# Graph-attention kernel: centring the linear weights 14 slots later in the last superblock of pass one, and spreading their sums from slot 42 to slot 66

## The chip, the cores and the metric

The kernel runs on one core of one Trainium2 chip. The metric is the time of one execution on the device, in microseconds (us). Before the change three runs gave 2664.1, 2664.25 and 2662.74 us, with a median of 2664.1 us.

## The reference

The input is x, 128 x 64 x 768, seen as 8192 tokens in 128 graphs of 64, and a 0/1 adjacency per graph. After a layer norm and a relu, two graph-attention layers follow. Everything is float32.

```python
for l in range(L):                                   # L = 2, H = 768
    m_left  = einsum('bsh,oh->bso', h, W_left[l])
    m_right = einsum('bsh,oh->bso', h, W_right[l])
    u_left  = einsum('bih,bjh->bij', h, m_left)  / sqrt(H)
    u_right = einsum('bih,bjh->bij', h, m_right) / sqrt(H)
    u = u_left * adj_tri + u_left * diag_mask + u_right * adj_tri.T
    e = exp(u) * adj
    attention = e / (e.sum(axis=2, keepdims=True) + 1e-10)
    h_lin = einsum('bsh,oh->bso', h, W_lin[l]) + b_lin[l]
    h = relu(layer_norm(matmul(attention, h_lin), ln_a[l], ln_b[l]))
return x + h
```

## The kernel before, in words

Each layer has two passes. **Pass one** multiplies the tokens by W_left and W_right, forms the scores and the softmax, and stores the attention. **Pass two** multiplies the tokens by W_lin, then by the attention, and normalizes. Both passes replace block products by a bilinear scheme with fewer products: sums of weight blocks times sums of token blocks, each product then added with signs into several outputs.

Pass one works through 32 parts of 256 tokens in 11 superblocks: the first of two parts, ten of three. One superblock after the first is 40 products (`PRODUCTS`), each of four matmuls at L658 into one of four PSUM banks in turn (names X, Y, Z, V or C, D, X, Y), so product i can start only when the reads of product i - 4 are done. The reads add each bank into the tiles m0, m1 and m2 (`READS`): the first write of a piece is a ScalarE activation (ACT) at L859, every later one a VectorE (DVE) operation at L245 or L863. After product 3 stand the score matmuls (L680) of the superblock before. The token sums that the products need (`T_OPS`, 38 of them, t9 to t46) are made one by one on GpSimd (POOL), at most 11 ahead of their use. L245 is the line of the helper `added`, so it stands for every addition on DVE and POOL; POOL and DVE additions on tiles g are sums of weights or tokens in SBUF, DVE additions on tiles m are reads of a bank.

The side work is put into a plan by slot: two slots per product, slot 2i while product i is issued and slot 2i + 1 behind its reads. `put(slot, f)` says at which slot f is written into the program; the engines then execute in their own order, each strictly in the order written. A slot is about 0.86 us when nothing waits.

In the **last superblock** of pass one (once in each layer), `final_of` adds the preparation of pass two to the plan:

- the nine blocks of W_lin are loaded (`load_n`, L214, slots 6 to 22), the first two token parts of pass two are loaded at slot 12, and the bias in three pieces (L901, slots 29 to 31);
- `centre` takes each row's mean out of W_lin, so that the layer norm of pass two needs no mean. The blocks go in three groups of three (j = 1, 0, 2), seven steps a group: for each block ACT copies the two halves onto themselves and accumulates their row sums (L233), DVE reduces the six sums and scales them (L228, L229), and ACT subtracts the mean from each block's halves (L237);
- `sums_n` makes the 17 weight sums of `W_SUMS` (n = 0 to 16), the even n on POOL, the odd n on DVE. Many work in place and so wait for each other across the two engines: n = 2 on POOL overwrites block 8, which n = 1 on DVE reads; n = 8 on POOL overwrites the block that n = 7 on DVE reads; n = 9 on DVE overwrites what n = 8 on POOL reads;
- the bias is summed, centred and combined at slots 40 to 60 (ACT L916, DVE L919 and L920, ACT L924, DVE L927 and L928, ACT L931);
- in the second layer ACT also applies scale, bias and relu to the first token parts (L379, 12 activations, slots 24 to 34);
- from slot 56 on POOL makes the 11 token sums of pass two (`put_sums_t`).

Around it stand the eight softmax steps of the superblock before at slots 10 to 31 (DVE L702 to L720, ACT L708), the last of which issues eight stores of the attention on the SP queue (L725), and the load of the next adjacency at slot 48, four DMA issues on ACT's own queue (L645).

Of the kernel before, what the change touches and what calls it, by code (L numbers as in the profile page):

```python
# [17 lines left out]
def kernel(  # L18
# [48 lines left out]
    def put(slot, *fs):  # L67
        plan.setdefault(slot, []).extend(fs)

    def put_all(slot, fs, step=1):  # L70
        for f in fs:
            if f is not None:
                put(slot, f)
            slot += step
        return slot
# [133 lines left out]
    def load_n(l):  # L209
        t = W[l, "n"] = {}  # L210

        def load(s, i, j):
            t[s] = free.popleft()
            nc.sync.dma_start(t[s], block_of("n", l, i, j))  # L214

        return [lambda s=s, ij=ij: load(s, *ij) for s, ij in RAW.items()]

    def centre(l):

        t = W[l, "n"]  # L220
        steps = []
        for j in (1, 0, 2):
            blocks = [s for s, (_, jj) in RAW.items() if jj == j]
            m = stat.tile([P, 3, K2], F32, name="wm", bufs=3)
            mean = stat.tile([P, K2], F32, name="wmm", bufs=3)

            def mean_of(m=m, mean=mean):
                nc.vector.reduce_sum(mean, m.rearrange("p n c -> p c n"), axis=mybir.AxisListType.X)  # L228
                nc.vector.tensor_scalar_mul(mean, mean, -1.0 / H)  # L229

            def sums(s, n, m=m):
                for c in range(K2):
                    nc.scalar.activation(t[s][:, c, :], t[s][:, c, :], AF.Copy, accum_out=m[:, n, c:c + 1])  # L233

            def less(s, mean=mean):
                for c in range(K2):
                    nc.scalar.activation(t[s][:, c, :], t[s][:, c, :], AF.Identity, bias=mean[:, c:c + 1])  # L237

            steps.extend([lambda n=n, s=s, sums=sums: sums(s, n) for n, s in enumerate(blocks)])
            steps.append(mean_of)  # L240
            steps.extend([lambda s=s, less=less: less(s) for s in blocks])
        return steps

    def added(eng, o, sign, a, b):
        (eng.tensor_add if sign == "+" else eng.tensor_sub)(o, a, b)  # L245

    def sums_n(l):
        t = W[l, "n"]

        def one(n, o, s, a, b):  # L250
            if o not in t:
                t[o] = free.popleft()
            added((nc.gpsimd, nc.vector)[n % 2], t[o], s, t[a], t[b])

        return [lambda n=n, x=x: one(n, *x) for n, x in enumerate(W_SUMS)]
# [27 lines left out]
    def put_sums_t(key, first, step, base):  # L283

        fs = sums_t(key)
        put_all(first, fs[:5], step)
        for f, s in zip(fs[5:], (21, 22, 23, 24, 25, 27)):
            put(max(base + s, first + 5 * step), f)
# [81 lines left out]
    def load_h(which, l, u, hold=False):  # L370
        for t in range(2):
            load_part(which, l, 2 * u + t, hold)
# [10 lines left out]
    def affine(which, l, u, step=1):  # L383
        return [lambda a=a, b=b: (a(), b()) for a, b in zip(*(affine_part(which, l, 2 * u + t, step) for t in range(2)))]
# [518 lines left out]
    def bias(l):  # L903


        ab = [free.popleft() for _ in range(2)]
        W[l, "bias"] = ab
        t = rows["bias", l] = [ab[n // 2][:, n % 2, :] for n in range(4)]
        todo = [lambda i=i, to=to: row(f"b{i}", b_lin[l], i * D, (i + 1) * D, t[to]) for i, to in enumerate((1, 2, 0))]
        bm = stat.tile([P, 3], F32, name="bm", bufs=1)  # L910

        bs = stat.tile([P, 1], F32, name="bs", bufs=1)

        def sums():
            for n in range(3):
                nc.scalar.activation(t[n], t[n], AF.Copy, accum_out=bm[:, n:n + 1])  # L916

        def mean():
            nc.vector.reduce_sum(bs, bm, axis=mybir.AxisListType.X)  # L919
            nc.vector.tensor_scalar_mul(bs, bs, -1.0 / H)  # L920

        def centred():
            for n in range(3):
                nc.scalar.activation(t[n], t[n], AF.Identity, bias=bs)  # L924

        def combined():
            nc.vector.tensor_add(t[1], t[1], t[0])  # L927
            nc.vector.tensor_add(t[3], t[1], t[2])  # L928

        def negated(n):  # L930
            nc.scalar.activation(t[n], t[n], AF.Copy, scale=-1.0)  # L931

        return todo, [sums, mean, centred, combined, lambda: negated(0), lambda: negated(2)]
# [322 lines left out]
    def final_of(l):  # L1256
        def final(slot, tokens):
            put_all(slot + 6, load_n(l), 2)
            put(slot + 12, lambda: load_h(2, l, 0))

            def rest():
                loads, work = bias(l)
                put_all(slot + 29, loads, 1)
                put_all(slot + 40, work, 4)

            put(slot + 28, rest)
            put_all(slot + 24, affine(2, l, 0), 2)
            put_all(slot + 14, centre(l), 1)
            put_all(slot + 30, sums_n(l), 2)
            put_sums_t((2, l, 0), slot + 56, 2, slot + 50)  # L1270
        return final

# [33 lines left out]
```

## Time and profile before

| | |
|---|---|
| median of 3 runs | 2664.1 us |
| profiled execution, its own time | 2660.78 us |
| span in the profile, first to last instruction | 2659.0 us |
| granted TensorE clock, mean | 0.996 |
| PE busy / DVE busy / POOL busy / ACT busy | 98% / 66% / 65% / 35% |
| last superblock, first layer | about 778 to 862 us |
| last superblock, second layer | about 2086 to 2169 us |

Views by time print one row per run of like instructions: start in us, duration in us, engine, line, operation, output <- input, count, and in square brackets how long the engine sat idle before it and which instruction released it. PE is the matrix engine. A product of four float32 matmuls stands there as eight records of 128x256. Views by group print busy time and mean ns of one, then the idle time before them. "issue" as a releaser means that no wait in the profile explains the idle time.

### The profile page before, as it was taken

To read this page: it belongs to the slowest core of one execution; us is meant where nothing else is said; L and a number is where in the kernel's file an instruction comes from. 1 tells how busy PE (TensorE), PEld (TensorE's weight loads), DVE (VectorE), ACT (ScalarE), POOL (GpSimd) and SP (SyncE) were. 2 spreads that over 40 slices of the span, in tenths; PEclk is the share of its full clock that TensorE was granted. 3 is DMA by queue.
4 is the path that set the end of the run, shared out by engine and by line. 5 is a ranking of instruction groups with operands and counts; after the bars stand their busy time and mean duration, and the time that the engine had idled before them with its cause. 6 is when DMAs were issued, how large, how long until landed. Compare 5 with 4: busy or idle time off the path is not lost. (4 is left out here: it accounts for less than half of the span.)

```text
span 2659.0 us, 46920 instructions
## 1 busy us (share of the span) xinstructions
PE 2602.9 (98%) x18042; PEld 2219.6 (83%) x18042; DVE 1753.8 (66%) x2840; ACT 934.3 (35%) x1963; POOL 1726.7 (65%) x1328
## 2 busy tenths in 40 slices
PE   9899999999999999999999999999999989999998
PEld 8788888888887788888788888888888878888886
DVE  7877787777768445554415676677666675666667
ACT  5522223223213254454542222222222425455453
POOL 4766676666668557776225666667666567878786
PEclk9999999999999999999999999999999999999999
DMA  7443534343421344446795524353542215565655
GB/s 219 111 112 87 123 92 113 92 116 78 100 62 52 123 148 151 163 136 215 203 287 137 130 60 111 77 128 93 133 100 69 66 49 150 160 172 159 182 159 146
DMA packets 263358, 336.52 MB, mean 127 GB/s; under 512 B 56290, under 2 KB 195298, under 8 KB 263138
## 3 DMA queue, kind: packets, MB, share of 16 engines
q1 hardware_dynamic: 246338, 325.28, 44.5%
q10 hardware_dynamic: 16800, 8.26, 1.2%
q8 instruction: 144, 2.36, 0.4%
q14 instruction: 76, 0.62, 0.1%
HBM read 218.11 MB, written 115.34 MB: 125 GB/s over the span
## 5 line engine op out<-in xcount | busy, mean ns | idle before, releaser
L245 POOL TENSOR_TENSOR g<-ht 128x512 f32<-128x512 f32 x584 | 769.1, 1327 | 474.4 <-ACT ht L379 117.6
L245 POOL TENSOR_TENSOR g<-g,g 128x512 f32<-128x512 f32 x295 | 381.9, 1303 | 140.1 <-DVE g L245 39.3
L245 POOL TENSOR_TENSOR g<-ht,g 128x512 f32<-128x512 f32 x256 | 338.1, 1328 | 156.3 <-PE X L658 40.0
L658 PE MATMUL C<-g,g 128*128 128x256 f32 x1008 | 241.1, 382 | 10.0 <-POOL g L245 8.0
L954 PE MATMUL Z<-g,g 128*128 128x256 f32 x1024 | 244.1, 380 | 2.8 <-ACT hl L300 2.7
L658 PE MATMUL X<-g,g 128*128 128x256 f32 x1008 | 241.3, 383 | 4.9 <-DVE m L863 4.8
L658 PEld LDWEIGHTS C<-g,g 128*128 128x128 f32 x1008 | 191.1, 191 | 39.3 <-POOL g L245 11.1
L658 PE MATMUL Y<-g,g 128*128 128x256 f32 x912 | 217.3, 381 | 3.8 <-POOL g L245 3.8
L954 PEld LDWEIGHTS Z<-g,g 128*128 128x128 f32 x1024 | 191.6, 190 | 35.1 <-issue 4.1
L379 ACT ACTIVATE ht<-ht,b_col,a_col 128x256 f32<-128x256 f32 x384 | 196.5, 592 | 67.5 <-DMA ht<-h 59.5
L658 PEld LDWEIGHTS X<-g,g 128*128 128x128 f32 x1008 | 192.0, 191 | 33.5 <-DVE m L863 5.6
L658 PE MATMUL D<-g,g 128*128 128x256 f32 x880 | 209.2, 381 | 3.2 <-POOL g L245 3.2
L658 PE MATMUL Z<-g,g 128*128 128x256 f32 x864 | 204.7, 380 | 0.0
L658 PEld LDWEIGHTS Y<-g,g 128*128 128x128 f32 x912 | 174.3, 191 | 28.1 <-POOL g L245 4.2
L245 DVE TENSOR_TENSOR m<-m,D 128x512 f32<-128x512 f32 x180 | 118.2, 677 | 117.6 <-ACT m L859 99.2
L658 PEld LDWEIGHTS D<-g,g 128*128 128x128 f32 x880 | 167.6, 191 | 27.0 <-POOL g L245 4.0
L658 PEld LDWEIGHTS Z<-g,g 128*128 128x128 f32 x864 | 163.5, 190 | 23.1
L954 PE MATMUL X<-g,g 128*128 128x256 f32 x768 | 182.7, 379 | 0.0
L658 PE MATMUL V<-g,g 128*128 128x256 f32 x768 | 181.4, 379 | 0.0
L1154 POOL TENSOR_TENSOR z<-z,b 128x768 f32<-128x768 f32 x62 | 112.7, 1829 | 81.7 <-DVE z L1151 77.2
L954 PEld LDWEIGHTS X<-g,g 128*128 128x128 f32 x768 | 145.7, 190 | 20.6 <-issue 0.6
L658 PEld LDWEIGHTS V<-g,g 128*128 128x128 f32 x768 | 145.9, 190 | 19.8
(224 smaller groups left out, 4661.9 us busy)
## 6 DMA issues: line engine op xcount, KB each, us to landing
ht<-h SPq DMA_DIRECT2D x126, 768.0 KB, 6.2
h<-xb SPq DMA_DIRECT2D x124, 384.0 KB, 6.5
z<-z SPq DMA_DIRECT2D x128, 192.0 KB, 3.1
x<-z SPq DMA_DIRECT2D x128, 192.0 KB, 5.4
xr<-in_x_dram SPq DMA_DIRECT2D x120, 192.0 KB, 3.8
out_dram<-xr SPq DMA_DIRECT2D x120, 192.0 KB, 2.7
x<-in_x_dram SPq DMA_DIRECT2D x112, 192.0 KB, 5.5
g<-form SPq DMA_DIRECT2D x40, 256.0 KB, 5.1
```

The source lines that it names most:

```text
L245: (eng.tensor_add if sign == "+" else eng.tensor_sub)(o, a, b)
L379: nc.scalar.activation(ht, ht, AF.Relu, bias=cols[1][:, c:c + 1], scale=cols[0][:, c:c + 1])
L658: nc.tensor.matmul(p[:, g], w[:, c, g * P:(g + 1) * P], t[:, c, :], start=(new and g == c == 0), stop=(c == K2 - 1), skip_group_check=True)
L954: nc.tensor.matmul(p[:, n], b[t][:, c, r * P:(r + 1) * P], w[s][:, c, :], start=(i in FIRST and i not in PRELOAD and n == c == 0), stop=(c ...
L1154: nc.gpsimd.tensor_add(zs[k], zs[k], rows["b"])
```

## The change

In both layers the 21 steps of `centre` move from slots 14 to 34 to slots 28 to 48. The 17 sums, before at every second slot from 30 to 62, now stand at slots 42, 43, 45, 46, 48, 49 and so on to 66.

```diff
             put(slot + 28, rest)
             put_all(slot + 24, affine(2, l, 0), 2)
-            put_all(slot + 14, centre(l), 1)
-            put_all(slot + 30, sums_n(l), 2)
+            put_all(slot + 28, centre(l), 1)
+            for n, f in enumerate(sums_n(l)):
+                put(slot + 42 + 3 * n // 2, f)
             put_sums_t((2, l, 0), slot + 56, 2, slot + 50)
```

No instruction is added or removed apart from regrouping; the 51 weight and token tiles g are handed out from a queue, so their numbers change from here on.

On POOL in the first layer's last superblock, these were the rows from the sum n = 0 (`g_119` is block 8, `g_153` block 12, `g_150` block 13) on; rows with ht are token sums or sums of token sums:

```order
L245 TENSOR_TENSOR g_163<-g_119,g_153 128x512
L245 TENSOR_TENSOR g_123<-ht,g_146 128x512
L245 TENSOR_TENSOR g_119<-g_119,g_150 128x512
L245 TENSOR_TENSOR g_143<-ht,g_129 128x512
L245 TENSOR_TENSOR g_157<-g_133,g_162 128x512
L245 TENSOR_TENSOR g_144<-ht 128x512
L245 TENSOR_TENSOR g_160<-g_152,g_121 128x512
```

With the change the same place on POOL reads:

```order
L245 TENSOR_TENSOR g_163<-ht,g_146 128x512
L245 TENSOR_TENSOR g_123<-ht,g_129 128x512
L245 TENSOR_TENSOR g_127<-ht 128x512
L245 TENSOR_TENSOR g_143<-g_152,g_121 128x512
L245 TENSOR_TENSOR g_157<-g_155,g_121 128x512
L245 TENSOR_TENSOR g_144<-g_119,g_153 128x512
L245 TENSOR_TENSOR g_160<-ht 128x512
L245 TENSOR_TENSOR g_151<-ht,g_130 128x512
L245 TENSOR_TENSOR g_119<-g_119,g_150 128x512
L245 TENSOR_TENSOR g_154<-ht,g_121 128x512
```

Before, the sum n = 2 (`g_119<-g_119,g_150`) stood behind token sum t35 and ahead of t36; now it stands behind t41, that is behind six more token sums, and n = 0 stands behind t39.

On DVE at the same time, in the difference (minus before, plus now), `g_142<-g_142,g_119` is the sum n = 1, `g_127<-g_163,g_150` and `g_135<-g_144,g_150` are n = 3 under its old and its new tile, `g_129<-g_147,g_162` is n = 7, and m rows are reads of banks:

```order
 L228 TENSOR_REDUCE wmm<-wm 128x2
 L229 TENSOR_SCALAR wmm<-wmm 128x2
-L245 TENSOR_TENSOR g_142<-g_142,g_119 128x512
 L863 TENSOR_SCALAR m_290<-C,m_290 128x8x64 x2
 L245 TENSOR_TENSOR m_290<-m_290,C 128x8x64
 L245 TENSOR_TENSOR m_288<-m_288,D 128x8x64
 L245 TENSOR_TENSOR m_290<-m_290,D 128x8x64
-L245 TENSOR_TENSOR g_127<-g_163,g_150 128x512
 L863 TENSOR_SCALAR m_290<-X,m_290 128x8x64
 L245 TENSOR_TENSOR m_290<-m_290,X 128x8x64
+L228 TENSOR_REDUCE wmm<-wm 128x2
+L229 TENSOR_SCALAR wmm<-wmm 128x2
```

The first pair L228, L229 is the mean of group j = 2 before and that of j = 1 now; n = 1 goes behind the reads of products 16 to 21, n = 3 behind those of product 22, and the means of j = 0 and j = 2 now stand between reads of products 18 and 23.

On ACT, these rows now stand between the centring of group j = 0 (`g_150`, `g_164`, `g_147`) and the read of product 25 (`m_289<-D`), the next bank read that ACT does:

```order
L916 ACTIVATE g_161,bm<-g_161 128x256 x2
L916 ACTIVATE g_122,bm<-g_122 128x256
L237 ACTIVATE g_147<-g_147,wmm 128x256 x2
L233 ACTIVATE g_133,wm<-g_133 128x256 x2
L233 ACTIVATE g_162,wm<-g_162 128x256 x2
L233 ACTIVATE g_128,wm<-g_128 128x256 x2
L237 ACTIVATE g_133<-g_133,wmm 128x256 x2
L237 ACTIVATE g_162<-g_162,wmm 128x256 x2
L645 DMA adj<-in_adj_dram 64x2x128 x2
L645 DMA adj<-in_adj_dram 64x4x128 x2
L237 ACTIVATE g_128<-g_128,wmm 128x256 x2
L924 ACTIVATE g_161<-g_161,bs 128x256 x2
```

Before, all of the centring stood ahead of the bias sums (L916) and of the four adjacency issues (L645); now the bias sums stand ahead of group j = 2, and the adjacency issues ahead of its last block.

## The prediction

> **What bounds the kernel now.** I read the page first: PE is busy 98% of the span, so only PE's waits can be won. Next came the timeline of PE. A superblock that nothing disturbs is the one ahead of the last in the first layer; these are its products 4 and 39.
>
> ```profile
> PE 2602.9 (98%) x18042; PEld 2219.6 (83%) x18042; DVE 1753.8 (66%) x2840; ACT 934.3 (35%) x1963; POOL 1726.7 (65%) x1328
> 716.23 1.99 PE L658 MATMUL X<-g,g 128*128 128x256 f32 x8
> 776.77 1.89 PE L658 MATMUL V<-g,g 128*128 128x256 f32 x8
> ```
>
> 35 products take 60.54 us, 1.73 each. In the last superblock the same products (first layer: 4, 20, 30, 39; second layer: 5, 20, 30, 39) stand so:
>
> ```profile
> 792.34 1.99 PE L658 MATMUL C<-g,g 128*128 128x256 f32 x8
> 821.70 1.99 PE L658 MATMUL C<-g,g 128*128 128x256 f32 x8 [1.47 <-POOL g L245]
> 843.44 3.65 PE L658 MATMUL X<-g,g 128*128 128x256 f32 x8 [2.38 <-DVE m L863]
> 860.77 1.89 PE L658 MATMUL Y<-g,g 128*128 128x256 f32 x8
> 2099.88 1.89 PE L658 MATMUL D<-g,g 128*128 128x256 f32 x8
> 2130.24 3.62 PE L658 MATMUL C<-g,g 128*128 128x256 f32 x8 [3.45 <-POOL g L245]
> 2151.97 1.99 PE L658 MATMUL X<-g,g 128*128 128x256 f32 x8 [2.37 <-DVE m L863]
> 2167.81 1.89 PE L658 MATMUL Y<-g,g 128*128 128x256 f32 x8
> ```
>
> First layer: 68.4 us for 35 products, 7.9 lost. Second: 67.9 for 34 where 58.8 would do, 9.1 lost. So **17.0 us** is all that this change can win. It is lost in two places: at product 20 for POOL, and at product 30, where bank X is still unread by DVE. After a wait PE sometimes runs one product at half speed (3.65 and 3.62 instead of 1.9), but not always (1.99).
>
> Why POOL is late is seen on POOL, DVE and ACT (POOL first layer, then second; then DVE):
>
> ```profile
> 819.15 1.27 POOL L245 TENSOR_TENSOR g<-g,g 128x512 f32<-128x512 f32 x1 [7.85 <-DVE g L245]
> 820.39 1.26 POOL L245 TENSOR_TENSOR g<-ht,g 128x512 f32<-128x512 f32 x1
> 2127.67 1.27 POOL L245 TENSOR_TENSOR g<-g,g 128x512 f32<-128x512 f32 x1 [10.67 <-DVE g L245]
> 817.99 0.12 DVE L228 TENSOR_REDUCE wmm<-wm 128x2 f32<-128x6 f32 x1
> 818.22 0.69 DVE L245 TENSOR_TENSOR g<-g,g 128x512 f32<-128x512 f32 x1
> ```
>
> By the order of rows, 819.15 is sum n = 2, 818.22 is n = 1, which it waits for, and n = 1 stands behind the mean of group j = 2 (817.99). Behind n = 2 is token sum t36 (820.39 to 821.65), and product 20 starts at 821.70. POOL idles 7.85 and 10.67 us, then runs without a gap, late.
>
> **The change part by part.** It adds no work. It moves 36 copies and subtractions on ACT, three means on DVE, nine sums on POOL and eight on DVE; it issues no DMA itself, and SP's queue keeps its order. The prices:
>
> ```profile
> L233 ACT ACTIVATE g<-g 128x256 f32<-128x256 f32 x18 | 7.2, 408 | 0.0
> 818.41 2.50 ACT L237 ACTIVATE g<-g,wmm 128x256 f32<-128x256 f32 x6 [0.65 <-DVE wmm L229]
> L379 ACT ACTIVATE ht<-ht,b_col,a_col 128x256 f32<-128x256 f32 x24 | 12.6, 598 | 0.0
> L229 DVE TENSOR_SCALAR wmm<-wmm 128x2 f32<-128x2 f32 x3 | 1.6, 549 | 0.1
> L245 DVE TENSOR_TENSOR g<-g,g 128x512 f32<-128x512 f32 x8 | 10.8, 1348 | 2.8 <-POOL g L245 2.8
> 864.13 2.47 DVE L245 TENSOR_TENSOR m<-m,X 128x512 f32<-128x512 f32 x4
> 866.52 2.47 DVE L245 TENSOR_TENSOR m<-m,Y 128x512 f32<-128x512 f32 x4
> ```
>
> A group's six copies take 2.4 us, its six subtractions 2.5, one L379 0.5 start to start, a read of a bank 0.60 (four in 2.39). A mean and its way back to ACT cost about 0.5 us, or 1.2 where L229 is slow. A DVE sum takes 0.69 us with POOL idle (818.22), 1.35 on average. A bank can be read 1.95 us after its product's start.
>
> *POOL.* Undisturbed, product i starts at 792.4 + 1.73 (i - 4). With the change t35 to t39 come ahead of every sum, then n = 0 once block 12 is centred, t40, t41, then n = 2, which still waits for n = 1. From this walk: ACT reads product 13, which starts at 808.0, three times by 811.4 and copies j = 1 by 813.8; DVE reaches the mean after the transposition at 815.7; ACT subtracts from 816.2 to 818.6 and copies j = 0 by 821.0. DVE waits for that from 820.2, reads products 19 to 21 by 824.4, and does n = 1 by 825.0. POOL then does n = 2 and t42 by 827.7, t43 by 829.0; products 26 and 27 want them at 830.4 and 832.2. **The wait at product 20 goes in both layers** (second layer: t42 at 2134.1 for 2136.2), with about 2 us to spare; if that cover is gone, product 26 waits for the excess.
>
> *DVE and ACT, the new path.* What is late next is bank X at product 30. Rows for it (ACT, ACT's DMA queue, then SP, then DVE):
>
> ```profile
> 826.61 0.42 ACT L916 ACTIVATE g<-g 128x256 f32<-128x256 f32 x1 [5.70 <-DMA g<-in_b_lin_dram]
> 828.08 1.28 ACTq L645 DMA_DIRECT2D adj<-in_adj_dram  x2
> 2052.22 1.58 ACT L379 ACTIVATE ht<-ht,b_col,a_col 128x256 f32<-128x256 f32 x3 [1.50 <-issue]
> 837.07 0.60 ACT L859 ACTIVATE m<-D 128x512 f32<-128x512 f32 x1 [6.17 <-DVE m L863]
> 818.10 5.09 SPq L725 DMA_DIRECT2D att<-wm  x8
> 823.23 0.59 SPq L901 DMA_DIRECT2D g<-in_b_lin_dram  x1
> 838.30 1.67 DVE L245 TENSOR_TENSOR g<-g,g 128x512 f32<-128x512 f32 x1
> 839.90 1.48 DVE L927 TENSOR_TENSOR g<-g 128x256 f32<-128x256 f32 x1
> 841.42 1.37 DVE L928 TENSOR_TENSOR g<-g,g 128x256 f32<-128x256 f32 x1
> 842.71 0.68 DVE L863 SCALAR_TENSOR_TENSOR m<-X,m 128x512 f32<-128x512 f32 x1
> ```
>
> The attention stores follow the transposition, now 2.3 us earlier, so the bias lands by about 824.4 (issue to use 3.4 before). ACT does the bias sums by 825.6, the last subtraction of j = 0 and the copies of j = 2 by 828.8. DVE, with the reads of product 22 done at 827.1, waits 1.7 us for them; behind that wait stand n = 3, the reads of 23 and 24, n = 5, done by 832.9. ACT subtracts two blocks by 830.9 and then issues four adjacency DMAs at 0.64 each. How long these hold ACT back is not shown for this place: nothing at best, 2.6 us at worst; 2052.22 shows 1.50 for the same four, and I take that. The last block and the bias follow, and ACT's read of product 25 ends at 835.1, where DVE has waited 2.2 us for it. Then n = 7 and the two bias additions (838.30 to 842.71 before: 4.4) and the read of bank X: done at 840.6 (839.5 to 841.7 by the bounds). **Product 30 starts at 840.7, not 843.44**, after a wait of 3.3 us.
>
> Behind it DVE has two sums more than before (n = 9 and n = 11 now stand there). 13 bank reads and four sums to the read of product 32 are 7.8 + 0.7 + 3 x 1.35 = 12 us, to 852.7. PE needs that bank for product 36; with one slow product (3.45) it gets there at 840.7 + 3.45 + 5 x 1.73 = 852.8. Product 36 thus starts at 852.8 for 855.6 (860.77 less 3 x 1.73): **2.8 us won.** From there the tail is the same chain of reads and score matmuls as before.
>
> *Second layer.* The same walk, 1305.7 us on. ACT has all twelve L379 (6 us) ahead of the copies of j = 0, which end at 2128.3, 1.6 later than in the first layer; but the bias has landed by then and costs no wait. Copies of j = 2 end at 2135.2, ACT's read of 25 at 2141.4, product 30 starts at 2146.9 (before 2151.97). With one slow product 36 starts at 2159.0 for 2162.6: **3.6 us won**, bounds 1.5 to 5.
>
> Sum: 6.4 us, by the bounds of ACT's hold and of the DVE sums (0.69 to 1.79) 2 to 10. The profiled execution took 2660.8 and would take 2654.4. The median shown is 3.3 above it, so **2657.7**.
>
> *Two rules weighed.* At 843.44 a wait of 2.38 brings a slow product, at 2151.97 one of 2.37 does not, at 2130.24 one of 3.45 does. The Trainium skill, TensorE: Matmul & The Clock Gate, section HAM oscillation, puts the limit for idle gaps near 3.4 us. By it my two waits of 3 us cost nothing, and the sum would be 7.3; the trace is split at 2.4, so I keep the slow products. The second rule speaks against the change. Rows 818.22 (0.69) and 838.30 (1.67) are the same DVE sum, with POOL idle and busy. The Trainium skill, SBUF — State Buffer, section Who interferes with whom, says that a DVE instruction with two SBUF inputs and a GpSimd one that reads SBUF exclude each other for a whole instruction. The trace agrees; its result is the first rival.
>
> **The rivals.**
> 1. *Sums collide.* Every sum on DVE now has a POOL sum within 1.5 slots. If each DVE sum and bias addition waits for a whole POOL operation, 0.69 + 1.27 = 2.0 instead of 1.35, the three ahead of bank X behind the last wait cost 1.5 us more, the three behind it 2.0. Per layer 1.5 to 2.5 of the gain go: 2 to 3 are left in all, 2662. For it: 1.67, 1.48 and 1.37 in a row. Against: POOL idles while n = 1, n = 3 and n = 9 run, since it waits for them or for ACT.
> 2. *ACT does not hold DVE.* If the adjacency issues run beside the activations and the bias lands early, the waits of 1.7 and 2.2 us on DVE shrink, no product is slow, and 10 to 12 us come back: 2653. Against: 2052.22.
> 3. *ACT becomes the bound, slower.* DVE's read of product 25 waits for ACT's, which now stands behind the centring of j = 2, four issues and the bias. Before, ACT idled 6.17 us there (837.07). Each us that ACT is later goes one to one into bank X, so the gain is gone when ACT is 3.2 us later than in my walk, the mean of 2.8 and 3.6. If the bias lands 5 us later than I put it and the issues hold 2.6 instead of 1.5, ACT is 6.1 us later in each layer: 12.2 less 6.4, 5.8 us slower, 2670. Against: the bias was in ACT's hands at 826.61 even behind later stores.
> 4. *No effect.* DVE is the true bound from product 20 on, since its row of reads and sums is as long as before, and the gain is within 1 us: 2664. For it: the wait of 2.38 on DVE survives in my own walk.
>
> **How the numbers follow.** Forecast 46%, rival 1 20%, rival 2 12%, rival 3 13%, rival 4 9%. 0.2%, about what a measurement of this kernel can tell from no change, is 5.3 us. Of the forecast's spread three quarters lie beyond that: with rival 2, 47% faster. Slower 13%, the rest 40%. The range runs from 2652 (rival 2) to 2664.5 (rivals 1 and 4 inside), leaving out rival 3 and a little of rival 2.
>
> **What would show it.** Right: no wait of PE for POOL at product 20; POOL's 7.85 and 10.67 gone, short POOL waits for DVE and ACT in their place; the one large wait left is product 30 for DVE, 2.5 to 4 us, starting by 841 and 2147; DVE waiting for ACT ahead of the L228 of j = 2 and ahead of the read of product 25. Wrong: a wait of PE for POOL at product 26, or product 30 starting after 843.4 and 2152.

## The result, and the profile after

The changed kernel took 2655.46 us (median of 7 runs, 2654.16 to 2656.76), the kernel before 2664.1 us beside it (7 runs, 2662.74 to 2664.95). The ratio is **0.9971, 95% interval 0.9960 to 0.9982**: 8.6 us less by the medians, 5 to 11 by the interval, faster by a little more than a measurement can tell. The profiled execution took 2654.31 us with a span of 2652.5, against 2660.78 and 2659.0 before, so 6.5 us of the gain are in the traces that are compared here.

The timeline of PE shows where. These rows are products 4, 20, 30 and 36 and the first product after the score matmuls, first layer and then second (there with product 31 too):

```profile
791.57 1.99 PE L658 MATMUL C<-g,g 128*128 128x256 f32 x8
819.30 1.89 PE L658 MATMUL C<-g,g 128*128 128x256 f32 x8
839.65 1.99 PE L658 MATMUL X<-g,g 128*128 128x256 f32 x8 [2.92 <-DVE m L863]
851.03 1.97 PE L658 MATMUL C<-g,g 128*128 128x256 f32 x8 [0.57 <-DVE m L245]
870.93 1.99 PE L954 MATMUL X<-g,g 128*128 128x256 f32 x8
2094.39 1.99 PE L658 MATMUL C<-g,g 128*128 128x256 f32 x8
2122.12 1.89 PE L658 MATMUL C<-g,g 128*128 128x256 f32 x8
2142.89 3.78 PE L658 MATMUL X<-g,g 128*128 128x256 f32 x8 [3.09 <-DVE m L863]
2146.47 3.15 PE L658 MATMUL Y<-ht,g 128*128 128x256 f32 x8
2156.36 1.89 PE L658 MATMUL C<-g,g 128*128 128x256 f32 x8
2174.80 1.99 PE L954 MATMUL X<-g,g 128*128 128x256 f32 x8
```

Product 20 no longer waits in either layer. Product 30 still waits for DVE, 2.92 and 3.09 us where it was 2.38 and 2.37. The program's other parts move the start of this stretch by a few us from run to run, so the measure used from here on is the **time from product 4 to the first product after the scores, both layers added**. For the changed kernel it is 79.36 + 80.41 = 159.8 us. For the kernel before, the rows that were not shown yet are the first product after the scores, then product 4 and the same for the second layer:

```profile
875.06 1.99 PE L954 MATMUL X<-g,g 128*128 128x256 f32 x8
2098.05 1.99 PE L658 MATMUL C<-g,g 128*128 128x256 f32 x8
2181.31 1.99 PE L954 MATMUL X<-g,g 128*128 128x256 f32 x8
```

82.72 + 83.26 = 166.0 us. So 6.2 of the profile's 6.5 us lie in these two stretches.

POOL after, the sums n = 0 and n = 2 in the first layer and n = 2 in the second:

```profile
817.15 1.28 POOL L245 TENSOR_TENSOR g<-g,g 128x512 f32<-128x512 f32 x1 [2.25 <-ACT g L237]
824.47 1.27 POOL L245 TENSOR_TENSOR g<-g,g 128x512 f32<-128x512 f32 x1 [3.58 <-ACT g L916]
2127.64 1.28 POOL L245 TENSOR_TENSOR g<-g,g 128x512 f32<-128x512 f32 x1 [3.36 <-ACT g L916]
```

The idle times of 7.85 and 10.67 us are gone, and shorter ones stand in their place, behind token sums that PE needs first. The two rows of n = 2 name ACT's bias sum as what ended the wait, but the bias sums touch no block that n = 2 uses; n = 1 on DVE, which it must wait for, ends at 824.24 in the first layer, 0.23 us ahead of it. On DVE in the first layer these rows lead to product 30 (n = 1, the mean of j = 2, a read of product 25's bank, n = 7, the two bias additions, the read of bank X):

```profile
823.56 0.68 DVE L245 TENSOR_TENSOR g<-g,g 128x512 f32<-128x512 f32 x1
827.98 0.16 DVE L228 TENSOR_REDUCE wmm<-wm 128x2 f32<-128x6 f32 x1 [1.66 <-ACT g L233]
833.81 0.69 DVE L245 TENSOR_TENSOR m<-m,D 128x512 f32<-128x512 f32 x1 [1.17 <-ACT m L859]
834.41 1.77 DVE L245 TENSOR_TENSOR g<-g,g 128x512 f32<-128x512 f32 x1
836.11 1.48 DVE L927 TENSOR_TENSOR g<-g 128x256 f32<-128x256 f32 x1
837.62 1.37 DVE L928 TENSOR_TENSOR g<-g,g 128x256 f32<-128x256 f32 x1
838.91 0.68 DVE L863 SCALAR_TENSOR_TENSOR m<-X,m 128x512 f32<-128x512 f32 x1
```

DVE waits twice for ACT, 1.66 and 1.17 us, and then has 4.5 us of sums (834.41 to 838.91) ahead of the read that product 30 waits for. On ACT, the first bias sum and the last two subtractions of j = 2:

```profile
823.45 0.42 ACT L916 ACTIVATE g<-g 128x256 f32<-128x256 f32 x1 [0.73 <-DMA g<-in_b_lin_dram]
831.19 0.91 ACT L237 ACTIVATE g<-g,wmm 128x256 f32<-128x256 f32 x2 [1.04 <-issue]
```

The bias DMA costs ACT 0.73 us and the four adjacency issues 1.04.

### The profile page after: what moved, and what is told of

Its sections match the earlier page's. It is cut to its first block, busy times and chain, and to the rows that moved or that the text cites. A ratio compares the mean times of both kernels' runs of the same rounds, so it can differ in the third digit from the quotient of the medians.

```text
span 2652.5 us, 46920 instructions
## 1 busy us (share of the span) xinstructions
PE 2600.1 (98%) x18042; PEld 2218.9 (84%) x18042; DVE 1751.0 (66%) x2840; ACT 934.9 (35%) x1963; POOL 1725.5 (65%) x1328
```

## The experiments

All kernels compute the whole reference; they differ only in what stands at which slot and on which engine. Ratios are to the kernel before, timed beside each. In the table, **waits** are what the product starts lose over the undisturbed pitch of 1.727 us, at products 17 to 24 and at 30 to 37, both layers added, losses under 0.2 us left out; **half clock** is what those of products 4 to 39 that PE ran at half its clock took beyond 1.94 us, and is taken out of the waits.

| kernel | waits 17–24 | waits 30–37 | half clock | measure | ratio (95%) |
|---|---|---|---|---|---|
| before | 7.7 | 5.1 | 3.4 | 166.0 | 1 |
| changed | 0 | 7.2 | 3.1 | 159.8 | 0.9971 (0.9960–0.9982) |
| changed, again | 0 | 7.4 | 1.7 | 158.0 | 0.9970 (0.9960–0.9980) |
| sums moved, centring not | 4.4 | 4.8 | 0 | 159.1 | 0.9979 (0.9971–0.9988) |
| centring and n = 0–2 old | 6.0 | 2.5 | 0 | 158.7 | 0.9979 (0.9970–0.9987) |
| centring and n = 0–7 old | 7.9 | 0 | 1.7 | 159.5 | 0.9978 (0.9968–0.9987) |
| before, additions on POOL at 58 | 7.7 | 0 | 1.8 | 158.9 | 0.9976 (0.9966–0.9985) |
| changed, additions on DVE at 66 | 0 | 8.0 | 0 | 159.9 | 0.9983 (0.9975–0.9992) |
| changed, additions on POOL at 52 | 0 | 6.4 | 3.2 | 158.7 | 0.9975 (0.9967–0.9983) |
| changed, bias from 50, additions on POOL, adjacency at 52 | 0 | 3.6 | 0 | 153.7 | 0.9950 (0.9938–0.9963) |
| the same, centring old | 4.4 | 1.5 | 0 | 155.8 | 0.9959 (0.9946–0.9971) |
| the same, adjacency old | 0 | 3.6 | 0 | 152.5 | 0.9950 (0.9937–0.9964) |
| the same, additions on DVE | 0 | 8.5 | 1.6 | 159.0 | 0.9973 (0.9963–0.9984) |

### The sums alone

The changed kernel with the centring back at its old slots:

```diff
-            put_all(slot + 28, centre(l), 1)
+            put_all(slot + 14, centre(l), 1)
```

> The 17 sums at slots 42 to 66 as in the change, the centring back at slots 14 to 34. Theory A (the loss before came from one wait on GpSimd: sum n = 2 for sum n = 1, with the token sums queued behind it; what is left is VectorE's row of reads and sums from product 19 to 36): the sums alone bring the whole gain. No PE wait for GpSimd at product 20; product 30 starts up to 1 us earlier than in the changed kernel, because ScalarE holds VectorE less there, though the bias sums land later (at 827 as before). Time 2653.5 us, 2651 to 2656.5. Rival B (the later centring matters, because ScalarE's bank reads ahead of it come earlier): less than half of the gain, 2659 to 2662.

Measured: 2656.32 us, ratio 0.9979 (0.9971 to 0.9988), measure 159.1. The time lies in theory A's range, but its account holds only in part. Product 20 no longer waits for POOL, yet products 17 to 24 still lose 4.4 us (7.7 before, none in the changed kernel), now mostly for DVE (0.7 of them for a read by ACT). Product 30 comes 0.7 and 1.0 us later behind product 4 than in the changed kernel, and not earlier. A softmax step on DVE and product 20, first layer:

```profile
817.23 1.36 DVE L716 TENSOR_TENSOR adj<-adj,s 128x384 f32<-128x384 f32 x1
824.25 1.97 PE L658 MATMUL C<-g,g 128*128 128x256 f32 x8 [0.55 <-DVE m L245]
```

With the centring at its old slots DVE waits 2.60 us for ACT's copies of j = 0, as it does in the kernel before. What is new is that POOL is now busy beside the softmax steps: L710, L714 and L716 take 1.01, 0.54 and 1.36 us, where they took 0.54, 0.17 and 0.56 beside the idle POOL of the kernel before, and take again in the next kernel, where POOL idles once more. DVE is 1.6 us later by that, and products 18 and 20 wait for its reads.

Products 30 to 37 lose 2.4 us less than in the changed kernel, and no product runs at half clock. By the measure the sums' new slots bring at least as much in this profile as the whole change; but 3.1 us of the changed kernel's 159.8 are half clock, and its second profile has 158.0. By time the changed kernel is ahead, 0.9971 and 0.9970 against 0.9979, with intervals that overlap. With the sums in their new slots the centring thus takes 4.4 us away at products 17 to 24, and the greater part comes back at products 30 to 37. No run moves the centring alone.

### The first three sums at their old place

```diff
-            put_all(slot + 28, centre(l), 1)
+            put_all(slot + 14, centre(l), 1)
             for n, f in enumerate(sums_n(l)):
-                put(slot + 42 + 3 * n // 2, f)
+                put(slot + 30 + 2 * n if n < 3 else slot + 42 + 3 * n // 2, f)
```

> Centring at slots 14 to 34 and the sums n = 0, 1, 2 at their old slots 30, 32, 34; the other 14 sums spread as in the change. Theory A: the idle time of GpSimd ahead of n = 2 is back (7 to 8 us in the first layer, 10 to 11 in the second), and so is PE's wait at product 20, about 1.5 and 3.4 us; product 30 then waits less, since VectorE needs the time anyway. Time 1 to 5 us above the kernel with all sums moved: 2657, 2655 to 2660. Rival (GpSimd was late because of the number of sums between slots 30 and 42, not because of one wait): no such idle time, no wait at product 20, time within 1 us of the kernel with all sums moved.

Measured: 2655.65 us, ratio 0.9979 (0.9970 to 0.9987), measure 158.7. Products 20 and 30 in the first layer, then in the second:

```profile
822.54 1.99 PE L658 MATMUL C<-g,g 128*128 128x256 f32 x8 [1.46 <-POOL g L245]
840.92 1.99 PE L658 MATMUL X<-g,g 128*128 128x256 f32 x8 [0.85 <-DVE m L863]
2127.72 1.99 PE L658 MATMUL C<-g,g 128*128 128x256 f32 x8 [3.44 <-POOL g L245]
2145.09 1.89 PE L658 MATMUL X<-g,g 128*128 128x256 f32 x8
```

The wait at product 20 is back as it was, 1.46 and 3.44 us, and the time is nevertheless no longer than with the sums alone, where I had expected 1 to 5 us more. A loss at product 20 alone cannot explain that. While PE waits there DVE catches up: product 30 waits for 0.85 us in the first layer and not at all in the second, instead of 1.60 and 1.31 with the sums alone and 2.92 and 3.09 in the changed kernel. So the gain need not come from product 20, and my account of it, which began there, is not enough. The view that the later runs test (A') is that **DVE's row of reads and sums ahead of product 30 and up to product 36** is what counts.

### The bias additions later, or on POOL

First the two additions on DVE moved behind product 32, to slot 66:

```diff
-                put_all(slot + 40, work, 4)
+                put_all(slot + 40, work[:3], 4)
+                put_all(slot + 66, work[3:], 4)
```

> The changed kernel with the two bias additions of VectorE (and the two negations behind them) moved from slots 52 to 60 to slots 66 to 74, behind the read of product 32. Theory A (VectorE's whole row of work up to product 36 is the bound, not the place of one item): the wait leaves product 30 (under 0.6 us) and comes back at products 36 and 37, 1.5 to 2.5 us in sum; time within 2 us of the changed kernel: 2655, 2653 to 2657. Rival C (only what stands ahead of bank X's read counts): 2.5 to 3 us won in each layer, 2650.

Measured: 2656.82 us, ratio 0.9983 (0.9975 to 0.9992), measure 159.9: no gain over the changed kernel. Product 30 waits for no more than 0.29 us, but products 32, 36 and 37 lose together what it no longer does (8.0 us against 7.2). The measure also holds 3.4 us at half clock among the score matmuls of the second layer, behind product 39 and so in neither column; they make these matmuls about 1.2 us longer. Moving work along DVE's row only moves the wait. Then the same additions given to POOL, at their old slot 52:

```diff
-            nc.vector.tensor_add(t[1], t[1], t[0])
-            nc.vector.tensor_add(t[3], t[1], t[2])
+            nc.gpsimd.tensor_add(t[1], t[1], t[0])
+            nc.gpsimd.tensor_add(t[3], t[1], t[2])
```

> The changed kernel with the two bias additions done on GpSimd instead of VectorE, same slot. Theory A: VectorE's row gets 2.85 us shorter, GpSimd has the room (it idles 2 to 3.6 us four times there); the wait at product 30 falls under 0.6 us, 1.5 to 2 us of waiting are left at product 36; 2.4 us won in the first layer, 2.5 to 5 in the second, where two products at half speed go with the wait. Time 2649.5, 2648 to 2652. Rival D (GpSimd is as short of time as VectorE, so that the token sums and weight sums behind the additions come late): a new wait of PE for GpSimd, time 2655 or more.

Measured: 2654.42 us, ratio 0.9975 (0.9967 to 0.9983), measure 158.7. That misses the 2649.5 that was expected by several us. POOL's rows from the additions on (the additions and n = 8), then DVE's n = 9 and its two reads of product 28's bank, and product 32:

```profile
840.39 0.73 POOL L927 TENSOR_TENSOR g<-g 128x256 f32<-128x256 f32 x1
841.20 0.72 POOL L928 TENSOR_TENSOR g<-g,g 128x256 f32<-128x256 f32 x1
841.89 1.26 POOL L245 TENSOR_TENSOR g<-g,g 128x512 f32<-128x512 f32 x1
```

```profile
843.18 1.73 DVE L245 TENSOR_TENSOR g<-g,g 128x512 f32<-128x512 f32 x1 [1.49 <-POOL g L245]
844.84 1.27 DVE L245 TENSOR_TENSOR m<-m,C 128x512 f32<-128x512 f32 x2
```

```profile
846.26 3.56 PE L658 MATMUL C<-g,g 128*128 128x256 f32 x8 [2.51 <-POOL g L245]
```

The two additions stand ahead of n = 8 on POOL. n = 9 on DVE starts as n = 8 ends (843.15). The reads that free bank C follow n = 9 and end at 846.11, and product 32, the next in that bank, starts 0.15 us behind them. The row names POOL, whose n = 10 happens to end at 846.27; but all that product 32 takes from POOL is the token sum t44, which was made by 837.5. So the wait left product 30 and came back at product 32, through a chain from POOL to DVE and on to PE.

### Only the end of the row relieved

If DVE's row is what counts, relieving it at product 30 alone must win as much as the change does, with the waits at product 20 untouched. Two kernels try it. One leaves the centring and n = 0 to 7 as before and moves only n = 8 to 16:

```diff
-            put_all(slot + 28, centre(l), 1)
+            put_all(slot + 14, centre(l), 1)
             for n, f in enumerate(sums_n(l)):
-                put(slot + 42 + 3 * n // 2, f)
+                put(slot + 30 + 2 * n if n < 8 else slot + 42 + 3 * n // 2, f)
```

> The changed kernel with the centring back at the old slots (14 to 34) and the sums n = 0 to 7 back at their old slots (30 to 44); only n = 8 to 16 stand at the changed kernel's slots (54 to 66). The measure is the time from product 4 to the first product after the score products, both layers added: 166.0 us before, 159.8 in the changed kernel. Theory A' (what counts is VectorE's row of reads and sums ahead of product 30's bank and on to product 36; a wait at product 20 is made good by then): the waits at products 20, 21 and 24 are there as before (about 1.6 and 3.6 us at product 20), product 30 waits for less than 0.5, the measure is 159 to 161, and the time is 5 to 7 us under the kernel before, a ratio of about 0.9976. Rival A (the loss is GpSimd's idle time and the wait at product 20): the waits at 20 and 21 stay lost, the measure is 163 to 166, and the ratio 0.999 to 1.

The other is the kernel before, with the additions of the bias on POOL, but later, at slot 58:

```diff
-            nc.vector.tensor_add(t[1], t[1], t[0])
-            nc.vector.tensor_add(t[3], t[1], t[2])
+            nc.gpsimd.tensor_add(t[1], t[1], t[0])
+            nc.gpsimd.tensor_add(t[3], t[1], t[2])
...
-                put_all(slot + 40, work, 4)
+                put_all(slot + 40, work[:3], 4)
+                put_all(slot + 58, work[3:], 4)
```

> The kernel before, its sums and its centring untouched; the two additions of the bias work go from VectorE to GpSimd, at slot 58, and the two negations behind them to slots 62 and 66. Theory A': product 30's wait of 2.5 us in each layer, and the half-speed product behind it (1.7), go, since VectorE's row ahead of it is shorter by the two additions; the waits at products 20, 21 and 24 stay; the measure (product 4 to the first product after the score products, both layers) goes from 166.0 to 159 to 160, a ratio of about 0.9975. Rival A: the wait at product 20 is untouched and with it nearly the whole loss, so at most 1 to 2 us are won, a ratio of 0.9992 to 1, and the wait at 30 comes back at 32 or 36.

Measured: 2656.97 us, 0.9978 (0.9968 to 0.9987), measure 159.5; and 2656.8 us, 0.9976 (0.9966 to 0.9985), measure 158.9. Both came out as DVE's row asks and against the view that product 20 is the whole loss. The second kernel's products 20 and 30, first layer:

```profile
824.93 1.99 PE L658 MATMUL C<-g,g 128*128 128x256 f32 x8 [1.46 <-POOL g L245]
844.12 1.89 PE L658 MATMUL X<-g,g 128*128 128x256 f32 x8
```

Product 20 waits as before, and product 30 not at all. So the kernel before had two losses, 7.7 us at products 17 to 24 and 5.1 at 30 to 37. The change removes the first and enlarges the second to 7.2; these two kernels remove the second and keep the first, and come out about alike.

### Both ends relieved

The changed kernel, with the bias work from slot 50 on, its additions on POOL (now at slot 62, behind n = 8, 10 and 12 there), and the adjacency load four slots later:

```diff
-                put(slot + 2 * SCORED + 42, lambda k=k: load_adj(k, nc.scalar))
+                put(slot + 2 * SCORED + (46 if k == last else 42), lambda k=k: load_adj(k, nc.scalar))
...
-            nc.vector.tensor_add(t[1], t[1], t[0])
-            nc.vector.tensor_add(t[3], t[1], t[2])
+            nc.gpsimd.tensor_add(t[1], t[1], t[0])
+            nc.gpsimd.tensor_add(t[3], t[1], t[2])
...
-                put_all(slot + 40, work, 4)
+                put_all(slot + 50, work, 4)
```

> The changed kernel with the bias work at slots 50, 54, 58, 62, 66 and 70, its two additions on GpSimd, and the last superblock's adjacency load of pass one issued at slot 52 in place of 48. Theory A': VectorE's row is shorter by the two additions (2.85 us), and what held ScalarE (0.73 for the bias DMA, about 1.2 for the bias sums, 1.04 of DMA issues) is out of the way of the copies and reads that VectorE waits for; no wait of over 0.6 at product 30, at most 1 us lost in each layer between products 4 and 39, the measure (product 4 to the first product after the score products, both layers) 151 to 154, a ratio of about 0.9948, 13 to 14 us under the kernel before. Rival: another row is late anyway (GpSimd, which gets the two additions, or ScalarE): the measure stays at 157 or more, and the wait is found at product 32 or 36.

Measured: 2650.57 us, **ratio 0.9950 (0.9938 to 0.9963)**, measure 153.7. Products 4, 30 and the first after the scores in the first layer, then 4, 30, 32 and the first after the scores in the second:

```profile
793.75 1.99 PE L658 MATMUL C<-g,g 128*128 128x256 f32 x8
838.75 1.89 PE L658 MATMUL X<-g,g 128*128 128x256 f32 x8
870.24 1.99 PE L954 MATMUL X<-g,g 128*128 128x256 f32 x8
2095.39 1.99 PE L658 MATMUL C<-g,g 128*128 128x256 f32 x8
2140.39 1.89 PE L658 MATMUL X<-g,g 128*128 128x256 f32 x8
2145.73 1.97 PE L658 MATMUL C<-g,g 128*128 128x256 f32 x8 [1.73 <-DVE m L245]
2172.60 1.99 PE L954 MATMUL X<-g,g 128*128 128x256 f32 x8
```

Product 30 waits in neither layer. What is left is mainly the wait at product 32 in the second layer, 1.73 us, for the same chain: n = 8 on POOL, n = 9 on DVE, then the reads of product 28's bank. That puts the second layer's loss, 2.6 us, above the 1 us a layer that I expected. Three kernels undo one part each.

The centring at its old slots:

```diff
-            put_all(slot + 28, centre(l), 1)
+            put_all(slot + 14, centre(l), 1)
```

> The kernel of the run before (changed kernel, bias work from slot 50 with its additions on GpSimd, adjacency load at slot 52; measure 153.7 us, product 4 to the first product after the score products, both layers) with one part undone: the centring is back at the old slots 14 to 34; the sums keep the changed kernel's slots. With the bias work in its old place the centring made no difference (159.1 without it, 159.8 with it), while about 1.65 us in the first layer and 2.76 in the second were lost at products 17 to 20. Theory 'one lag' (a wait at product 20 is made good only as long as a later wait, at product 30, can shrink for it): here there is no wait at 30 left, so those 4.4 us at products 17 to 20 come on top, less what product 32's 2.2 gives back: the measure is 155.5 to 158 and the time 2 to 4 us longer than with the new centring, a ratio to the kernel before of about 0.996. Rival (the centring's place never counts): no more than 0.8 us from 153.7, a ratio of about 0.995.

The adjacency load at its old slot:

```diff
-                put(slot + 2 * SCORED + (46 if k == last else 42), lambda k=k: load_adj(k, nc.scalar))
+                put(slot + 2 * SCORED + 42, lambda k=k: load_adj(k, nc.scalar))
```

> The kernel with the bias work from slot 50 and its additions on GpSimd, with one part undone: the adjacency load of the last superblock is issued at slot 48 again, so that its four issues hold ScalarE for about 1 us ahead of the copies of j=2. Theory A' (VectorE's row of sums counts, ScalarE's hold only as far as VectorE waits for it): VectorE waits up to 1 us longer for the copies of j=2 and has slack at product 30, so 0 to 1 us more in each layer, a measure of 153.7 to 155.5, a ratio of 0.995 to 0.9957. Rival (ScalarE's hold is what was lost at product 30): the wait at product 30 is back at 1 to 2 us, a measure of 156.5 or more, a ratio of about 0.996.

The additions back on DVE:

```diff
-            nc.gpsimd.tensor_add(t[1], t[1], t[0])
-            nc.gpsimd.tensor_add(t[3], t[1], t[2])
+            nc.vector.tensor_add(t[1], t[1], t[0])
+            nc.vector.tensor_add(t[3], t[1], t[2])
```

> The kernel with the bias work from slot 50 and the adjacency load at slot 52, with one part undone: the two additions of the bias work are back on VectorE (at slot 62, some 2.85 us of its row). Theory A': the additions stand behind product 30's bank now, so product 30 waits for less than 0.6, but the row up to product 36 is as long as in the changed kernel: 1.5 to 3 us are lost in each layer at products 32 to 37, a measure of 156 to 158.5, a ratio of about 0.9963. Rival (it was ScalarE's hold, not VectorE's row): the measure stays at 153 to 155 and the ratio at 0.995.

Measured: 2652.21 us (0.9959), 2650.61 us (0.9950) and 2657.03 us (0.9973); measures 155.8, 152.5 and 159.0. The centring is worth 2.1 us of the measure here: it takes 4.4 us away at products 17 to 24 and gives 2.1 back at 30 to 37. By time the difference is 1.6 us, within the intervals. The adjacency load's place makes no difference, although ACT is held by it as before, 1.09 us. The additions on DVE cost 5.3 us of the measure, a little more than expected: the waits at products 32 to 37 grow by 4.9 us and 1.6 us of half clock are added, while what follows product 39 is 1.1 us shorter. In the first layer of that kernel the two additions, the reads of bank Y behind them and product 35 stand so:

```profile
844.95 1.48 DVE L927 TENSOR_TENSOR g<-g 128x256 f32<-128x256 f32 x1
846.53 1.30 DVE L928 TENSOR_TENSOR g<-g,g 128x256 f32<-128x256 f32 x1
847.76 1.27 DVE L245 TENSOR_TENSOR m<-m,Y 128x512 f32<-128x512 f32 x2
```

```profile
849.09 1.99 PE L658 MATMUL Y<-g,g 128*128 128x256 f32 x8 [2.12 <-DVE m L245]
```

Product 35 starts as soon as bank Y is read, behind 2.8 us of additions. This pair shows that the additions in DVE's row, and not the adjacency load's hold on ACT, kept the rest of the gain from the changed kernel. What the later bias sums on ACT (slot 50 instead of 40) add is not separated: no run gives the late additions to POOL with the bias sums at slot 40 in the changed kernel.

### The changed kernel once more

> The changed kernel, unaltered, beside the others of this call, for a second profile and a ratio on the same chip. All theories: a ratio of 0.996 to 0.9982 and a measure of 158 to 161 us (product 4 to the first product after the score products, both layers). What it shows is how far the half-speed products are chance: behind the wait of about 3 us at product 30 there were none in the first layer and two in the second; if it is chance, their number differs here (0 to 2 in either layer) while the wait at product 30 stays at 2.9 to 3.1.

Measured: 2655.79 us, ratio 0.9970 (0.9960 to 0.9980), measure 158.0. Product 30 waits 3.06 and 3.09 us, so the waits repeat. Again no product of the first layer is slow and two of the second are, but the half-clock time does not repeat: 1.7 us here and 3.1 in the first profile. The granted clock (the column ahead of the last two, PEclk) in the changed kernel's first profile and in this one, second layer, in stretches of 1 us from product 30 on:

```profile
2142.00:2143.00 1.00, 0.10 (x1) 0.59 0.00 0
2143.00:2144.00 1.00, 1.00 (x3) 0.50 0.00 0
...
2148.00:2149.00 1.00, 1.00 (x3) 0.50 0.00 0
2149.00:2150.00 1.00, 1.00 (x6) 1.00 0.00 0
```

```profile
2149.00:2150.00 1.00, 1.00 (x4) 0.68 0.00 0
2150.00:2151.00 1.00, 1.00 (x4) 0.50 0.00 0
...
2152.00:2153.00 1.00, 1.00 (x4) 0.61 0.00 0
```

A stretch at 0.68 was at half clock for 0.64 us. So the second took 0.64 + 1 + 1 + 0.78 = 3.42 us at half clock, and the first 0.82 + 6 = 6.82, twice as much; it began while PE still waited, 0.7 us ahead of product 30 (2142.89). Two neighbouring products share one such spell, or two spells follow each other.

## Why the prediction was right

The forecast was a gain of 6.4 us, 2657.7; the profiled execution was put at 2654.4 and took 2654.31. By medians the gain was 8.6, with 5 to 11 in the interval, so 6.4 lies inside. The mechanism held up to product 30: POOL's wait goes, and DVE's row is what is late next. That the profiled time fits to 0.1 us is luck; the same kernel's second profiled execution took 2658.45. Times below are on the changed trace, with the first layer's offset of 0.77 us (product 4 at 791.57 instead of 792.34) added.

- **The loss that could be won.** 17.0 us; the table finds 16.2 above the pitch before, and 10.3 after.
- **Product 20.** "The wait at product 20 goes in both layers": it did. Of the 7.7 us lost at products 17 to 24 not all was for POOL: 0.7 us at product 17 in the second layer was a wait for a read by ACT, and it went too. n = 1 on DVE ends at 825.0 (forecast 825.0), n = 2 starts at 825.2, the token sum behind it ends at 827.7 (827.7). No product waits for POOL at 26.
- **ACT and DVE on the new path.** The bias is used from 824.2 (824.4); copies of j = 2 end at 828.7 (828.8); DVE waits 1.66 for them (1.7). Only the adjacency issues were too dear: ACT was held for 1.04 us and not 1.5, and DVE waited 1.17 for the read of product 25 and not 2.2.
- **Product 30.** 840.4 in place of 840.7. In the second layer, with its offset of 3.66, 2146.55 in place of 2146.9. The sums ahead of the read took 4.5 us (forecast 4.4).
- **Product 36.** Forecast 852.8 and 2159.0; it came at 851.8, 1.0 us early, and at 2160.0, 1.0 late. Early, because 11 bank reads stand behind bank X and not the 13 that I counted, about 1.2 us too many. Late, because the second layer got 3.05 us of half clock where I had put one slow product, 1.7, and the first layer none. The two errors cancel by luck: 3.8 + 2.6 = 6.4 us at product 36, as forecast (2.8 + 3.6), and 6.2 behind the scores.
- **The clock rule.** I kept the slow products against the limit of 3.4 us that the Trainium skill gives (TensorE: Matmul & The Clock Gate, HAM oscillation). Of 14 waits from 2.11 to 3.45 us between products 4 and 39, 9 were followed by half clock; without the four of 3.44 and 3.45, 6 of 10. The shortest was 2.11. Among the score matmuls one of 1.86 us was followed by it too (additions on DVE at 66, second layer), and in the first layer of that kernel one of the same length was not; no other spell falls between product 4 and the first product after the scores in any of these profiles. The trace does not agree with 3.4 us as a bound for harmless waits here. The same page's Part 1, The HAM clock gate, has a window of about 3.4 us that runs freely; the 3.42 and 6.82 us at half clock agree with that. The 7.3 that the prediction gives for the sum by the limit does not follow from its walk: without slow products DVE's row still holds product 36 to about 852.7 in the first layer, so the sum would be about 6.6.
- **Rival 1, sums collide.** The DVE sums next to busy POOL take 1.77 and 1.79 us, those next to idle POOL 0.68, but there are no more slow ones than before: the ten sums and additions between products 16 and 39 take 12.8 us in the first layer against 13.6. Collisions do cost time at a place that the rival did not name, DVE's softmax steps in the kernel with the sums alone (1.6 us in a layer).
- **Rival 2, ACT does not hold DVE.** True in part, 1.0 us in the first layer. Making ACT's path freer still, by the adjacency load, brought nothing.
- **Rival 3, ACT becomes the bound.** It needed 3.2 us more on ACT than my walk; ACT was 0.6 us earlier.
- **Rival 4, DVE is the true bound.** Not from product 20 on, but from product 30 on it is what holds the rest. The runs show that it was so before too: taking 2.85 us off DVE's row there, with product 20 left waiting, wins about as much as the change.

What the prediction did not see is that the two losses partly exchange. Of the 4.4 us that the centring's move takes from products 17 to 24 with the sums in their new slots, 2.4 come back at products 30 to 37, and in the changed kernel's profiles 1.7 to 3.1 us of half clock follow that longer wait.

## What to carry to other kernels

When PE loses time at two places of one stretch and the same engine's row leads to both, relieving the first can lengthen the wait at the second, as it did here: walk the row to the end of the stretch before counting the gain, and relieve both. Move work off the late engine instead of along it, and place it on the other engine behind the operations that the late engine waits for: on POOL ahead of n = 8 the two additions of this kernel brought a wait of 2.5 us at product 32 in each layer, and behind n = 12, in a kernel with the bias sums later too, none at that size. The releaser that a row names is inferred: where an operation waits for several, look up which of them it needs and when that one ended. A second profile of the same kernel tells which losses belong to it and which, like the half-clock spells, vary.

## What was not expected of the hardware

- Half-clock spells after PE waits come in lengths of 3.42 us (changed kernel again; 3.4 also with the additions on POOL at slot 52) or twice that, 6.82. A spell of 3.4 us costs 1.6 to 1.8 us while PE is busy, whether it falls on one product (3.56 instead of 1.97) or is spread over two (2.78 and 2.83 instead of 1.94).
- Waits of nearly the same length go both ways: 3.06 us left the clock full (first layer, the changed kernel again) and 3.09 halved it (second layer); 2.12 and 2.11 likewise in the two layers of the kernel with the additions back on DVE.
- Where POOL was idle, DVE's step L716 (128x384, two inputs) took 0.56 us; beside a busy POOL in the kernel with the sums alone it took 1.36.
- The two bias additions took 1.48 + 1.37 us on DVE and 0.73 + 0.72 on POOL (additions at slot 52), where POOL's own sums of twice the width take 1.27.
- Four DMA issues on ACT's queue, about 0.6 us each, held ACT's activations for 1.04 us, not for the 2.5 that the issues last.
